# One sum of x1's blocks given to VectorE earlier in each turn: ahead of the tanh products instead of behind the gate's last sums

## The chip, the cores and the metric

The kernel runs on one core of a Trainium2 chip (trn2). The metric is the device time of one execution in microseconds (us), as the median over several runs. Engines are named as in the profile: PE is TensorE's matmul, PEld its weight load, DVE is VectorE, ACT is ScalarE, POOL is GpSimd, SP is SyncE, which issues the DMAs here. L240 is line 240 of the kernel.

## The reference, cut to what matters

Two layers of a graph network over 128 graphs of 64 nodes, with 768 features, all in float32:

```python
# layer 0: 12 heads of 64 features
h    = einsum('bnd,ade->bane', x, W)
th   = tanh(h)
attn = leaky(th @ w_src + transpose(th @ w_dst));  masked by adj;  softmax
out  = elu(einsum('banm,bame->bane', attn, h) + b)
gate = sigmoid(x @ H_w.T + H_b)
x1   = layernorm(x + gate * out + (1 - gate) * x)
# layer 1: 6 heads of 128 features
q, k, v = x1 @ Wq + bq, x1 @ Wk + bk, x1 @ Wv + bv
y    = softmax(q k^T / sqrt(128), masked by adj) v @ Wf + bf
x    = layernorm(x1 + y)
```

## The kernel before, in words

**Tiles and pairs.** A tile is 128 rows, that is two graphs. Layer 0 works on pairs of tiles, 32 pairs in all. A pair's two tiles are called t0 (first) and t1 (second) where the pair is the old one, n0 and n1 where it is the new one. Layer 1 begins when the last pairs are through.

**Products in seven parts.** Each product of a pair with a 768 x 768 weight (`h` for the features of layer 0, `g` for its gate, `v` for the values of layer 1) is done as a 2 x 2 block product with seven block products in place of eight. They are numbered 1 to 7, so `v6` is block product 6 of the values. Some of them take sums of the operand's blocks. For the values the operand is x1, transposed (tile `x1T`, 128 partitions x 6 chunks x 256 rows; the columns up to 128 are t0, those behind are t1). With a11 and a12 the two halves of t0's features and a21, a22 those of t1, `block_sums` makes four sums on DVE, each 128x384 float32:

```python
            lambda: e.tensor_tensor(s1, a21, a22, ALU.add),        # L240
            lambda: e.tensor_tensor(s2, s1, a11, ALU.subtract),    # L241
            lambda: e2.tensor_tensor(s3, a11, a21, ALU.subtract),  # L242
            lambda: e2.tensor_tensor(s4, a12, s2, ALU.subtract),   # L243
```

The first sum, s1, takes t1 alone. The second, s2, takes t0 too, and it is the stationary operand of `v6`. s1 itself is that of `v5`. In the profile the four are `sv_v`; the same lines run on POOL for the input x of layer 0, there they are `sx_x`.

**The order of the work is written out by hand.** The kernel runs under a manual schedule: each engine executes its instructions in the order in which they are emitted, and waits for the others where data demand it. A turn of the main loop takes a new pair through `h` and `g` and the old pair (one behind) through the rest of layer 0 and the values. `TURN` is the order of the block products on PE in one turn, 21 positions from 0 to 20:

```python
TURN = [
    "h1", "h2", "u4", "u3", "h6", "g1", "h5", "h7", "g2", "g6", "h4",
    "h3", "g5", "g7", "v1", "v2", "g4", "v6", "g3", "v5", "v7",
]
```

(`u4` and `u3` are the values' last two block products of the pair before the old one.) `step` emits a block product and behind it the way out of the one before, the DVE or ACT instructions that take it from PSUM. Other work is put on positions: `was(pos, ...)` for the old pair, `at(pos, ...)` for the new. What has the same position is emitted in the order of the calls. Turns 0, 1 and 2 and the tail have other tables of positions (`FIRST_AT`, `SECOND_OLD`, `THIRD_AT`, `LAST_AT`); turns 3 to 31, 29 in all, take the positions as written.

**The steps of a turn that matter here**, with their positions:

- 8: `by_features(t1)` transposes x1 of t1 on PE and copies it into `x1T` on ACT (L966, L967). 11: the same for t0.
- 11: `products(n1)`, 12: `products(n0)`: tanh of h on ACT (L888), then a product with w_dst on DVE (L889) and one with w_src on POOL (L890).
- 13, 14: `terms` sums these per head on DVE (`sd`, L897), writes the result to DRAM (`dstd`, L899) and reads it back spread over the rows (`dd`, two DMAs, L902); `with_bias` adds a bias to h on POOL (L913) and moves parts of it by DMA (L918, L919).
- 12: `v_begins` names the operands of the values and the four sum tiles; it issues no instruction.
- 15: s1, s2, and the DMA that writes `x1T` to DRAM (L1055). 16: s3, and `logits(n1)`, which adds `dd` and `sd` on DVE (L926, `att`). 18: `masked(n1)` (L942 to L949) and `logits(n0)`. 19: s4 and `exps(n1)`. 20: `masked(n0)`.
- Early in the next turn: `exps` on ACT (L955), transposes of the probabilities on PE (`pTp`), `attend` (L987), and `features` on DVE (L1003, L1004), which frees the PSUM banks for the transposes of the other tile.
- In between POOL makes the sums of the next x (`sx_x`) and sums of weights for layer 1 (`wacc`, L366), a few in each turn.

Of the kernel before, what the change touches and what calls it, by code (L numbers as in the profile page):

```python
# [134 lines left out]
def kernel(  # L135
# [620 lines left out]
    with ExitStack() as ph, ExitStack() as ph_r:  # L756
# [349 lines left out]
        v_sums, carried = {}, {}  # L1106
        summing = sum_weights(sb)
        for p in range(NP + 1):
            q = p - 1
# [9 lines left out]
            def at(pos, ok, *acts, places=of_new):  # L1119
                if ok:  # L1120
                    plan.setdefault(places.get(pos, int(pos)), []).extend(acts)

            def was(pos, *acts):
                at(pos, old, *acts, places=of_old)

            def do(f, *args):
                return lambda: f(*args)
# [15 lines left out]
            was(7.5, do(gated, t0))  # L1143
            was(8, do(by_features, t1), do(stats, t0))
            was(9, do(normed, t0))
            was(12, do(v_begins))
            was(15, lambda: v_sums[q][0](), lambda: v_sums[q][1](), do(spill_features, q))
            was(16, lambda: v_sums[q][2]())
            was(19, lambda: v_sums[q][3]())

# [210 lines left out]
```

## Time and profile before

| what | value |
|---|---|
| median of 3 runs | 2896.88 us (2893.63 to 2897.95) |
| the profiled execution | 2895.01 us |
| its span | 2893.2 us |
| mean granted TensorE clock | 0.998 |
| PE busy | 2842.0 us (98%) |
| DVE busy | 1939.4 us (67%) |
| POOL busy | 1292.9 us (45%) |
| ACT busy | 1059.4 us (37%) |
| share of PE in the chain that ended last | 78% |
| share of DVE in that chain | 11% |

The profile is of one execution, 1.8 us shorter in its span than that execution's own time. Layer 0 fills about the first 1535 us of the span. A view of waits says which instruction an idle engine waited for; a view of the timeline gives start, length, engine, line, output and inputs of each instruction, with the idle time before it in brackets.

### The profile page before, as it was taken

How to read it: one execution, taken by the hardware profiler on the slowest of the kernel's cores; microseconds unless marked ns; L12 is line 12 of the kernel's file. 1: busy time of each engine (PE TensorE's matmuls, PEld its weight loads, DVE VectorE, ACT ScalarE, POOL GpSimd, SP SyncE). 2: the span in 40 equal slices, each digit the busy share in tenths (PEclk: the TensorE clock that was granted, in tenths of full speed). 3: DMA queues.
4: the chain of work that ended last, by engine and by line, in shares of the span. 5: the costliest groups of instructions: out<-in, count | busy, mean ns of one | idle time of the engine just before them, and what ended most of it. 6: DMA issues, size and time to landing. Idle time of an engine off the chain costs nothing.

```text
span 2893.2 us, 47876 instructions
## 1 busy us (share of the span) xinstructions
PE 2842.0 (98%) x18252; PEld 2072.5 (72%) x18252; DVE 1939.4 (67%) x3203; ACT 1059.4 (37%) x1896; POOL 1292.9 (45%) x1253
## 2 busy tenths in 40 slices
PE   8899999999999999999999999999999999999998
PEld 4565556666566556666668888888888888888886
DVE  7878888888878888787863545555545555554556
ACT  2444444444344444444433223333213333322332
POOL 3445444444545444233343445434545443444534
PEclk9999999999999999999999999999999999999999
DMA  5444444444444444333353434332223433223432
GB/s 181 132 154 145 140 145 146 152 154 150 135 153 156 136 150 138 112 116 105 126 199 89 123 96 111 109 90 80 84 80 111 110 102 93 70 84 94 110 88 74
DMA packets 322068, 348.73 MB, mean 121 GB/s; under 512 B 147888, under 2 KB 247216, under 8 KB 321840
## 3 DMA queue, kind: packets, MB, share of 16 engines
q1 hardware_dynamic: 321840, 345.66, 39.2%
q8 instruction: 146, 2.39, 0.4%
q14 instruction: 82, 0.67, 0.1%
HBM read 198.48 MB, written 122.29 MB: 111 GB/s over the span
## 4 chain that ended last, share of the span: by engine, by line
PE 78%; DVE 11%; DMA 3%; issue 3%; ACT 3%; POOL 2%; SPq 0%; POOLq 0%; DVEq 0%; ACTq 0%
PE z_k L447 9%; PE z_o L494 9%; PE z_q L447 8%; PE y_h L270 6%; PE y_k L447 6%; PE y_q L447 6%; PE y_o L494 6%; PE y_g L270 5%; PE y_v L270 5%; PE z_h L270 3%; PE z_v L270 3%; PE z_g L270 2%; PE sp L550 2%; PE cp L634 2%; DVE sd L897 2%
## 5 line engine op out<-in xcount | busy, mean ns | idle before, releaser
L574 ACT ACTIVATE sc<-sc 128x512 f32<-128x512 f32 x48 | 30.6, 638 | 615.2 <-DVE sc L571 615.2
L695 POOL TENSOR_TENSOR y<-y,bf_bc 128x768 f32<-128x768 f32 x64 | 114.7, 1813 | 290.5 <-DMA y<-x1d 290.5
L507 DVE TENSOR_TENSOR y<-y,z_o 128x256 f32<-128x256 f32 x320 | 127.3, 417 | 140.4 <-PE z_o L494 140.2
L494 PE MATMUL z_o<-wf,so 128*128 128x256 f32 x896 | 215.8, 383 | 2.3 <-DVE y L507 1.2
L447 PE MATMUL z_q<-xs,w_wq 128*128 128x256 f32 x896 | 213.5, 381 | 0.3 <-POOL xs L411 0.3
L411 POOL TENSOR_TENSOR so<-ctxT 128x256 f32<-128x256 f32 x224 | 159.8, 731 | 90.8 <-PE y_o L494 45.9
L447 PE MATMUL z_k<-xs,hw_wk 128*128 128x256 f32 x840 | 198.5, 379 | 0.0
L1017 POOL TENSOR_TENSOR x<-gate,x 128x768 f32<-128x768 f32 x64 | 119.3, 1865 | 152.0 <-ACT gate L1068 137.0
L494 PEld LDWEIGHTS z_o<-wf,so 128*128 128x128 f32 x896 | 167.2, 190 | 26.9 <-issue 2.0
L447 PEld LDWEIGHTS z_q<-xs,w_wq 128*128 128x128 f32 x896 | 168.7, 190 | 24.3 <-POOL xs L411 0.7
L322 POOL TENSOR_TENSOR rs_b<-ve_b,minus_half 128x1 f32<-128x1 f32 x64 | 40.4, 631 | 313.0 <-DVE ve_b L320 312.2
L890 POOL TENSOR_TENSOR th<-th,wsd 128x768 f32<-128x768 f32 x64 | 117.9, 1843 | 134.6 <-DVE th L889 133.7
L447 PEld LDWEIGHTS z_k<-xs,hw_wk 128*128 128x128 f32 x840 | 159.5, 190 | 21.7
L322 POOL TENSOR_TENSOR rs_a<-ve_a,minus_half 128x1 f32<-128x1 f32 x64 | 35.8, 560 | 309.9 <-DVE ve_a L320 309.9
L411 POOL TENSOR_TENSOR xs<-r,r 128x512 f32<-128x512 f32 x112 | 147.4, 1333 | 40.3 <-DMA r<-x1Td 28.9
L462 DVE TENSOR_TENSOR qT<-qT,z_q 128x512 f32<-128x512 f32 x96 | 65.9, 687 | 141.5 <-PE z_q L447 141.5
L270 PE MATMUL y_v<-wv,sv_v 128*128 128x384 f32 x384 | 136.3, 491 | 10.3 <-DVE sv_v L241 8.3
L270 PE MATMUL y_h<-w_wq,xT 128*128 128x384 f32 x384 | 136.5, 492 | 8.5 <-DMA w_wq<-in_w_dram 7.9
L462 DVE TENSOR_TENSOR kT<-kT,z_k 128x512 f32<-128x512 f32 x96 | 66.0, 687 | 112.8 <-PE z_k L447 110.7
L270 PE MATMUL y_v<-wv,x1T 128*128 128x384 f32 x384 | 137.4, 495 | 1.8 <-ACT x1T L967 1.0
L270 PE MATMUL z_h<-w_wq,sx_x 128*128 128x384 f32 x384 | 137.6, 495 | 0.2 <-DVE w_wq L216 0.2
L270 PE MATMUL z_v<-wv,sv_v 128*128 128x384 f32 x384 | 137.6, 495 | 0.0
(165 smaller groups left out, 6909.0 us busy)
## 6 DMA issues: line engine op xcount, KB each, us to landing
x<-in_x_dram SPq DMA_DIRECT2D x64, 384.0 KB, 3.7
dd<-dstd SPq DMA_DIRECT2D x128, 192.0 KB, 3.4
x1d<-x SPq DMA_DIRECT2D x64, 384.0 KB, 2.6
x1Td<-x1T SPq DMA_DIRECT2D x32, 768.0 KB, 4.4
vd<-v SPq DMA_DIRECT2D x64, 384.0 KB, 3.0
r<-x1Td SPq DMA_DIRECT2D x96, 256.0 KB, 3.5
v<-vd SPq DMA_DIRECT2D x384, 64.0 KB, 2.3
y<-x1d SPq DMA_DIRECT2D x64, 384.0 KB, 5.4
```

The costliest lines, as they stand in the source:

```text
L270: T.matmul(to[:, : self.n], lhsT, rhs, start=kc == 0 and not more, stop=kc == HK - 1, skip_group_check=more,)
L322: G.tensor_tensor(rstd, ve, minus_half, ALU.pow)
L411: G.tensor_tensor(t, self.of(x[0]), self.of(x[2]), x[1])
L447: T.matmul(b[:, half * W2 : (half + 1) * W2], w[:, kc, half * P : (half + 1) * P], x[:, kc, :], start=half == kc == 0 and not more, stop=k ...
L462: V.tensor_tensor(at, at, b.rearrange("p (h t) -> p h t", h=2), ALU.add if sign > 0 else ALU.subtract,)
L494: T.matmul(b[:, :W2], x[:, kc, :], w[:, kc, :], start=kc == 0 and not more, stop=kc == 1, skip_group_check=more,)
L507: V.tensor_tensor(at, at, self.banks[path][:, :W2], ALU.add if sign > 0 else ALU.subtract)
L550: T.matmul(self.sp_[gr * N : (gr + 1) * N, (i * 2 + a) * N : (i * 2 + a + 1) * N], qT[:, 2 * self.f + a, at], kT[:, 2 * self.f + a, at], s ...
L634: T.matmul(self.cp_[a][e, at], self.v_[rows, i, gr, e], self.scT_[rows, at], start=True, stop=True,)
L695: G.tensor_tensor(y, y, pools["bf"], ALU.add)
L890: G.tensor_tensor(th[:, 1, :], th[:, 1, :], wsd[:, 1, :], ALU.mult)
L1017: G.tensor_tensor(xp, st[t]["gate"], xp, ALU.mult)
```

## The change

One line of the turn's plan is split. The naming of the operands and s1 go to position 11, and since the call stands ahead of the call that puts `products(n1)` there, s1 is emitted ahead of it. s2 and the write of `x1T` stay at position 15.

```diff
             was(9, do(normed, t0))
-            was(12, do(v_begins))
-            was(15, lambda: v_sums[q][0](), lambda: v_sums[q][1](), do(spill_features, q))
+
+            was(11, do(v_begins), lambda: v_sums[q][0]())
+            was(15, lambda: v_sums[q][1](), do(spill_features, q))
             was(16, lambda: v_sums[q][2]())
```

The calls behind it stay as they are: `at(11, new, do(products, n1))`, then `was(11, do(by_features, t0))`. In turn 1 `SECOND_OLD` sends position 11 to 15 and position 15 to 16, in turn 2 `THIRD_AT` takes 2 from each position, and in the tail `LAST_AT` sends 11 to 12 and 15 to 15.

## The prediction

> **What bounds the kernel now.** I read the page first. Its first part says that PE is the bound:
>
> ```profile
> PE 2842.0 (98%) x18252; PEld 2072.5 (72%) x18252; DVE 1939.4 (67%) x3203; ACT 1059.4 (37%) x1896; POOL 1292.9 (45%) x1253
> ```
>
> So an edit on DVE can only win what PE still waits for. The view of PE's waits in the first 1550 us (layer 0) has this at its top (total us, times, longest):
>
> ```profile
> PE y_v L270 <- DVE sv_v L241: 8.3, 11, 1.7
> ```
>
> That is v6 waiting for s2, the largest wait of PE there. For DVE the same view shows where DVE itself is idle:
>
> ```profile
> DVE th L889 <- ACT th L888: 98.0, 62, 2.8
> ...
> DVE att L926 <- DMA dd<-dstd: 10.0, 6, 5.0
> ```
>
> The first is the product that the change puts s1 in front of: DVE sits idle before it, 98 us in 62 cases. The second will come back as a limit. Next the view of the sums' tile (ns: shortest, median, longest):
>
> ```profile
> L240 DVE TENSOR_TENSOR sv_v<-x1T x32: 811/1309/2005, 89.1 to 1518.1; 128x384 f32<-128x384 f32 x32
> L241 DVE TENSOR_TENSOR sv_v<-sv_v,x1T x32: 557/965/1921, 90.5 to 1519.1; 128x384 f32<-128x384 f32 x32
> L242 DVE TENSOR_TENSOR sv_v<-x1T x32: 541/549/883, 91.0 to 1521.9; 128x384 f32<-128x384 f32 x32
> ```
>
> The three are the same operation on the same shape, yet s1 (L240) takes 1.31 us and s3 (L242) 0.55. The timeline of one turn, DVE and then POOL, tells why (start, length, idle before):
>
> ```profile
> 720.82 0.55 DVE L866 TENSOR_TENSOR gate<-y_g,hb_bc 128x384 f32<-128x384 f32 x1
> 723.43 0.96 DVE L889 TENSOR_TENSOR th<-th,wsd 128x768 f32<-128x768 f32 x1 [2.07 <-ACT th L888]
> ...
> 729.74 1.74 DVE L897 TENSOR_REDUCE sd<-th 128x24 f32<-128x1536 f32 x1
> 731.40 1.77 DVE L240 TENSOR_TENSOR sv_v<-x1T 128x384 f32<-128x384 f32 x1
> 733.20 0.56 DVE L241 TENSOR_TENSOR sv_v<-sv_v,x1T 128x384 f32<-128x384 f32 x1
> ...
> 734.62 1.52 DVE L926 TENSOR_TENSOR att<-dd,sd 128x768 f32<-128x768 f32 x1
> ```
> ```profile
> 720.62 0.73 POOL L366 TENSOR_TENSOR wacc_k<-wacc_k,wadd_k 128x256 f32<-128x256 f32 x1
> ...
> 729.43 3.32 POOL L913 TENSOR_TENSOR h<-h,b_bc 128x768 f32<-128x768 f32 x2
> ```
>
> POOL's two L913 end at 732.75, and s1, begun at 731.40, ends at 733.17, 0.42 us later. So s1 stood still until POOL was through. At 721.37, where the change puts it, DVE has 2.06 us of idle time and POOL has just finished.
>
> **Part 1: s1 at its new place.** 32 instructions move, none is added, and no DMA: the write of x1T stays on position 15, so SP's queue keeps its order, and so do POOL's, ACT's and PE's. On DVE s1 passes both L889, h's way out (L851), both L897 and the way outs L866 and L867. Its waits: x1T of t1, copied by ACT by 718.71 in this turn, and the old s1's last reader, v5 of the turn before; both are past. Queued behind it is L889 of n1, which needs ACT's tanh, ended at 723.40. I read this gap in every turn: from turn 2 to turn 31 it is 1.86 to 2.76 us, and POOL has at most one L366 of 0.73 us in it. So s1 costs 0.55 there, at worst 0.55 + 0.73 = 1.28, below the smallest gap: nothing. In turn 1 it falls into an idle 3.09 us ahead of L926 (waiting for `dd`). In the tail it falls among the way outs of layer 1's query (L462), where DVE waits for PE. If the cover were gone, it would cost 0.55 to 1.3 us a turn.
>
> **Part 2: s2 takes s1's place.** s2 starts when s1 did. Is it then done 1.3 us earlier? No: POOL's L913 still runs. Having s1's shape, s2 should end where s1 ended, so it comes earlier by its own length, 0.56 to 1.92 us. (In the Trainium skill, "SBUF — State Buffer", section "Who interferes with whom", a DVE instruction with two SBUF inputs and a GpSimd instruction that reads SBUF exclude each other for a whole instruction, and whoever comes second waits. By that rule the wait is inherited by s2, which the row of 733.17 bears out; were s1 simply a slow instruction, s2 would win s1's whole length, and the sum below would be about 1 us larger.)
>
> For v6 I took from PE's timeline the distance between starts of consecutive block products in the 29 full turns and subtracted the smallest of the 29. Ahead of v6 the excess is 0.49, 0.70, 0.71, 0.42, 0.13, 0.79, 1.87, 0.69, 0.10, 1.16, 0.54 and 0.19 us in twelve turns, 7.8 in all; turns 1 and 2 wait 1.13 and 1.38. With s2 ending where s1 ended and v6 starting 0.15 behind it (as the waiting ones do), all is gone but 0.88 of the 1.87, where s1 itself ended late, at 780.74:
>
> ```profile
> 781.88 2.17 PE L270 MATMUL y_v<-wv,sv_v 128*128 128x384 f32 x6 [1.71 <-DVE sv_v L241]
> ```
>
> and 0.47 and 0.11 of turns 1 and 2. That is 7.8 + 2.5 - 1.5 = **8.8 us**. In 23 turns v6 is also 0.08 longer than other products (1.9 in all), since its weights, which are s2, can't be loaded ahead; I count 1.4 of it. PE wins **10.2 us** at v6.
>
> **Part 3: what is late next.** The largest other excess in PE's table lies at the transposes of t0's probabilities in the next turn: 0.14 in nearly every turn, up to 1.55 in some, 8.8 in all. That chain runs L926 of n1, leaky, L942 to L949, L926 of n0, ..., L955 on ACT, L851, L1003, L1004, and DVE is nearly gapless in it. If PE comes earlier and the chain doesn't, the transposes wait longer. The chain comes earlier by s2's length at most, but L926 can't start before `dd` lands. From the issues of `dd` and their times to landing (3.0 to 3.8 us) I get a lead for each turn, the time from landing to L926: in this turn it landed at 734.51, L926 began at 734.62. 15 of 29 turns have 0.35 or less. With excess after = the larger of 0.14 and (excess + won at v6 - lead), and n0's `dd` as a second limit:
>
> - given back, named by v6's time: 0.32 (226), 0.78 (319), 0.51 (412), 0.37 (688), 0.99 (782), 0.54 (1012), 0.12 (1059), 0.26 (turn 1): 3.9 us;
> - kept: turn 2 and those at 366, 828, 1104, whose lead is 0.8 us or more, and the last full turns, which have 0.14 there;
> - won in turns without a wait at v6, by the lead alone: 0.9 us.
>
> **The sum.** 10.2 - 3.9 + 0.9 = **7.2 us**. The profiled execution took 2895.0 (span 2893.2 and 1.8 around it), so 2887.8 on its own scale. The median shown is 2896.88, 1.9 above it; the forecast against it is 2896.88 - 7.2 = **2889.7 us**. The unknown sizes: s2 at its new place 0.55 (POOL idle) to 2.0 (s1's longest), which moves the sum by about 1 up and 2 down; the lead used from nothing to all. I take s1's end, the nearest row. The sum can't exceed 10.2 plus what stands at the transposes above 0.14 (4.8): 15 us.
>
> **The rivals.**
>
> *Given back at the transposes.* If dependence on `dd` is tighter than my leads say, what v6 wins is lost 20 us later. For it: in six turns DVE already waits for `dd`. Against it: leads of 0.6 to 1.7 us in turns with waits of 0.7 us and more (v6 at 366, 688, 828, 1012). With no lead used only some 1 us stays; with a third to a half of the leads, 3. Time 2893.9 (2891 to 2896).
>
> *The move reaches nothing.* s2 needs t0's copies as well; if these, not s1, held it, nothing would change: 2896.9. Against it: they end at 725.17, six us ahead of s2.
>
> *Slower: L926 lands in POOL's sums.* L926 too reads two SBUF tiles and takes 1.52 us beside an idle POOL and 2.24 beside the `sx` sums. With s1 gone from POOL's way the `sx` sums start earlier. In 17 of the 29 turns L926 of n1 still takes 1.52. If an `sx` sum is under way whenever `dd` lands, each pays 0.72: 12.2 us, and these turns' gain goes too; 4.5 stay elsewhere. 2896.9 + 12.2 - 4.5 = 2904.6. It decides from the point at which `sx` starts ahead of the landing. Against it: in most of these turns POOL then waits for a DMA of weights and has no `sx` sum to run.
>
> **How the numbers follow.** Forecast 0.55, given back 0.26, nothing 0.07, slower 0.12. A measurement of this kernel can tell about 0.2% from no change, that is 5.8 us: faster is below 2891.1, slower above 2902.7. Nearly all of the forecast (0.50) and a little of the second case (0.04) make faster 0.54; most of the slower case makes slower 0.10; 0.36 is left for the same. The range reaches from 2885 (most of the leads kept, no wait inherited) to 2900, into the slower case; some 0.05 lie below it and 0.12 above.
>
> **What would show it.** Step 1: L240 at 0.55 us in the gap ahead of L889, and L889 no later behind the tanh; wrong if L240 takes over 1 us there. Step 2: L241's median near s1's old 1.3 us, and the wait y_v on L241 down from 8.3 to some 1.5. Step 3: PE's excess at the transposes up by about 3 us, and more waits of L926 for `dd`. The forecast is wrong if that excess grows by 8 or more, or if L926 has its 2.24 us in more turns than before.

## The result, and the profile after

The changed kernel takes 2885.29 us (median of 7 runs, 2883.43 to 2890.02) against 2894.46 for the kernel before in the same rounds (7 runs, 2892.59 to 2897.95): ratio 0.9967, 95% interval 0.9958 to 0.9976, that is 9.2 us less (6.9 to 12.2 by the interval). 7.2 were forecast. The forecast time, 2889.7, is 4.4 too high, and the measured one lies at the lower end of the range: 2.4 of the 4.4 come from the kernel before, whose median over all seven runs is 2894.46 and not the 2896.88 of the first three, and 2.0 from the change being worth more than forecast. The prediction put that lower end at most of the leads kept and no wait inherited by s2. s2 does inherit the wait (below), so the time came near this end for other reasons.

PE's waits in the first 1550 us of the changed kernel (total us, times, longest), those of interest:

```profile
PE pTp L966 <- DVE rden L1003: 3.5, 5, 1.1
...
PE pTp L966 <- DVE fo L1004: 1.7, 10, 0.2
...
PE y_v L270 <- DVE sv_v L241: 1.0, 2, 0.7
```

v6's wait for s2 went from 8.3 to 1.0 us. The wait of the transposes (pTp) for DVE's `rden` grew; in the kernel before the same view has

```profile
PE pTp L966 <- DVE rden L1003: 1.2, 2, 1.0
```

DVE's own waits in the same stretch, in the changed kernel:

```profile
DVE th L889 <- ACT th L888: 86.5, 62, 2.3
...
DVE att L926 <- DMA dd<-dstd: 24.1, 29, 4.1
```

The idle time ahead of L889 shrank by 11.5 us, s1 now stands in part of it, and L926 waits for `dd` 29 times instead of 6. The sums' tile, changed kernel (ns: shortest, median, longest):

```profile
L240 DVE TENSOR_TENSOR sv_v<-x1T x32: 546/548/1540, 83.8 to 1503.9; 128x384 f32<-128x384 f32 x32
L241 DVE TENSOR_TENSOR sv_v<-sv_v,x1T x32: 814/1314/1998, 88.5 to 1509.4; 128x384 f32<-128x384 f32 x32
```

s1 fell from 1.31 to 0.55, s2 rose from 0.97 to 1.31: the wait for POOL changed its owner. The same turn as in the prediction, DVE and then POOL:

```profile
717.62 0.55 DVE L240 TENSOR_TENSOR sv_v<-x1T 128x384 f32<-128x384 f32 x1
719.78 0.96 DVE L889 TENSOR_TENSOR th<-th,wsd 128x768 f32<-128x768 f32 x1 [1.62 <-ACT th L888]
...
727.75 1.77 DVE L241 TENSOR_TENSOR sv_v<-sv_v,x1T 128x384 f32<-128x384 f32 x1
...
731.10 1.52 DVE L926 TENSOR_TENSOR att<-dd,sd 128x768 f32<-128x768 f32 x1 [0.65 <-DMA dd<-dstd]
```
```profile
725.78 3.33 POOL L913 TENSOR_TENSOR h<-h,b_bc 128x768 f32<-128x768 f32 x2
```

L240 lies in the gap with 1.62 us of idle time to spare behind it, and L889 is still released by ACT. L241 has the 1.77 us that L240 had, and ends 0.41 after POOL's two L913 (729.11; DVE 729.52). L926, which began 0.11 after its landing before, now stands 0.65 us waiting for it.

Layer 0 got faster by the whole 9.3 us: the first product of layer 1's query starts at 1480.2 us instead of 1489.5. Of that 5.0 remain in the profiled execution at the start of the last such product (2806.2 instead of 2811.2). That execution took 2890.02, the longest of the seven; 1.8 of what it lost is PE waiting for ACT (`cp`, 3.1 us instead of 1.3), the rest was not followed up. In the profiles below, layer 1 takes 1322 to 1325 us between the starts of its first and last `y_q` product, here 1326.

### The profile page after: what moved, and what is told of

Read it like the earlier page. It is cut to its first block, busy times and chain, and to the rows that moved or that the text cites. A ratio compares the mean times of both kernels' runs of the same rounds, so it can differ in the third digit from the quotient of the medians.

```text
span 2888.2 us, 47874 instructions
## 1 busy us (share of the span) xinstructions
PE 2840.2 (98%) x18252; PEld 2075.9 (72%) x18252; DVE 1924.9 (67%) x3203; ACT 1061.2 (37%) x1896; POOL 1303.5 (45%) x1253
## 4 chain that ended last, share of the span: by engine, by line
PE 80%; DVE 9%; DMA 4%; ACT 3%; issue 2%; POOL 1%; SPq 1%; POOLq 0%; DVEq 0%; ACTq 0%
PE z_k L447 9%; PE z_o L494 9%; PE z_q L447 8%; PE y_h L270 6%; PE y_g L270 6%; PE y_k L447 6%; PE y_o L494 6%; PE y_q L447 5%; PE y_v L270 5%; PE z_h L270 4%; PE z_v L270 3%; PE z_g L270 2%; PE cp L634 2%; PE sp L550 2%; PE x_g L270 2%
## 5 line engine op out<-in xcount | busy, mean ns | idle before, releaser
L890 POOL TENSOR_TENSOR th<-th,wsd 128x768 f32<-128x768 f32 x64 | 118.0, 1844 | 137.7 <-DVE th L889 137.7
```

The lines of the kernel that those rows point to most:

```text
L890: G.tensor_tensor(th[:, 1, :], th[:, 1, :], wsd[:, 1, :], ALU.mult)
```

## The experiments

All ratios are to the kernel before, with 95% intervals. "Excess" is the measure of the prediction: the distance of block products on PE above the smallest of the 29 full turns. Before, it was 9.9 us at v6 (7.99 ahead of it and 1.89 within) and 8.8 at the transposes; in the changed kernel 2.1 and 10.0.

**Theory.** s1 costs nothing in the gap; s2 inherits the wait for POOL but ends earlier by its own length; what PE wins at v6 is in part given back at the transposes because L926 cannot start before `dd` has landed. **Rivals.** The early naming of the tiles is part of the gain; s1 does cost something where it stands; the place does not matter as long as s1 is gone from in front of s2; the landing of `dd` does not matter.

**The naming alone** (e1_names_only):

```diff
-            was(11, do(v_begins), lambda: v_sums[q][0]())
-            was(15, lambda: v_sums[q][1](), do(spill_features, q))
+            was(11, do(v_begins))
+            was(15, lambda: v_sums[q][0](), lambda: v_sums[q][1](), do(spill_features, q))
```

> Only the naming of the operands (with the four sum tiles) goes to position 11; s1 stays at position 15. My theory (the gain comes from s1's instruction alone, which now runs in an idle gap of VectorE): no instruction moves, so the time is that of the kernel before, ratio 1.000 within 0.001, and PE's wait of y_v on L241 stays near 8 us. Rival (taking the tiles earlier changes which waits are emitted, and that is part of the gain): ratio 0.998 or lower with L240 still at 1.3 us.

Ratio 1.0001 (0.9992 to 1.0010); v6 waits 8.7 us for s2, L240 has its 1.31. The gain is s1's instruction alone.

**s1 twice, at both places** (e3_s1_twice):

```diff
-            was(15, lambda: v_sums[q][1](), do(spill_features, q))
+            was(15, lambda: v_sums[q][0](), lambda: v_sums[q][1](), do(spill_features, q))
```

> s1 is computed twice, at position 11 as in the changed kernel and again at position 15 as before it (the same sum is written twice). My theory (s1 at the new place costs nothing, all of the change is that s1 is gone from position 15): ratio to the kernel before 1.000 within 0.001, the second L240 at 1.3 us as before, L889 of n1 still released by ACT. Rival (s1 at position 11 does delay the tanh products or POOL, and the gain at v6 is net of that): ratio 1.001 to 1.004, by the 0.55 us that it would cost in up to 29 turns.

Ratio 1.0000 (0.9992 to 1.0009). DVE executes 32 sums more than before, and the time does not move. The view of waits of this kernel, DVE and then PE:

```profile
DVE th L889 <- ACT th L888: 82.3, 62, 2.1
```
```profile
PE y_v L270 <- DVE sv_v L241: 7.2, 10, 1.4
```

The idle time ahead of L889 fell from 98.0 to 82.3 us, since the added sums of 0.55 us stand in its place, and v6 waits 7.2 us again. s1 in the gap is free.

**No s1 at all** (e4_no_s1; s2 is a21 - a11, and v5 multiplies a21, so the values are others):

```diff
+            B[q][5] = t[:, :HK, P:]
+            s2 = B[q][6]
+            v_sums[q][1] = lambda: V.tensor_tensor(s2, t[:, :HK, P:], t[:, :HK, :P], ALU.subtract)
```

> s1 is left out altogether: s2 is computed from a21 alone, and v5 takes a21 in its place, so the values are those of another product. My theory (the gap hides s1 fully): the same time as the changed kernel, ratio to the kernel before 0.996 to 0.998. Rival (s1 still costs something where it stands now): ratio 0.995 or lower, up to 0.55 us in each of 32 turns less than the changed kernel, that is 0.991 at the lowest.

Ratio 0.9971 (0.9960 to 0.9982), the changed kernel's within the intervals. Both sides agree within the intervals, which reach some 3 us to either side: adding s1 in the gap costs nothing, and taking it out of the gap wins nothing that they can tell. (In the one profiled execution layer 1 begins 1.7 us earlier than in the changed kernel's, at 1478.5 instead of 1480.2.)

**s1 behind the tanh products of n1 instead of ahead** (e2_s1_behind):

```diff
-            was(11, do(v_begins), lambda: v_sums[q][0]())
+            was(11, do(v_begins))
...
             at(11, new, do(products, n1))
+            was(11, lambda: v_sums[q][0]())
```

> s1 at position 11 as in the changed kernel, but emitted behind the tanh products of n1 instead of ahead of them. My theory (it is the idle gap ahead of L889 that makes s1 free, and POOL's L890, which starts when L889 ends, holds s1 up behind it): L240 has a median of 1.5 to 2 us instead of 0.55, L851 and the next L889 wait behind it, L897 of n1 begins 0.4 to 0.8 us later behind L889 of n1 than 3.6, dd lands that much later, and the ratio to the kernel before is 0.999 to 1.003: the gain is lost. Rival (any place ahead of L897 will do, VectorE has idle time ahead of the second L889 too): ratio 0.997 as for the changed kernel.

Ratio 0.9978 (0.9968 to 0.9987): some two thirds of the gain stay, so the expectation that it is lost was wrong. The interval alone would also allow the rival's 0.997; in the profiles layer 1 begins at 1483.6 us, 5.9 earlier than before the change, where the changed kernel's begins 9.3 earlier. DVE, then POOL, in this kernel:

```profile
723.56 0.96 DVE L889 TENSOR_TENSOR th<-th,wsd 128x768 f32<-128x768 f32 x1 [2.09 <-ACT th L888]
724.44 0.55 DVE L240 TENSOR_TENSOR sv_v<-x1T 128x384 f32<-128x384 f32 x1
...
727.41 1.74 DVE L897 TENSOR_REDUCE sd<-th 128x24 f32<-128x1536 f32 x1
```
```profile
724.60 2.07 POOL L890 TENSOR_TENSOR th<-th,wsd 128x768 f32<-128x768 f32 x1 [3.15 <-DVE th L889]
```

I had expected POOL's L890 to hold s1 up. It is the other way round: L240 stands directly behind L889 on DVE and is first, POOL comes 0.16 us later and takes 2.07 us instead of 1.82. L897 then starts 3.85 us behind L889 in most turns instead of 3.60, and `dd` lands 0.25 later behind L889 too, as the median of the 43 landings (of 58) that can be read; single ones move by up to 1.1 us either way. The place does matter, by a quarter of a microsecond a turn and not by 0.4 to 0.8.

**`dd` replaced by a tile that is always there** (e5a_before_dd on the kernel before, e5b_after_dd on the changed one; the DMAs still run, layer 0's attention is computed from other numbers):

```diff
-            sd, dd = st[t].pop("sd"), st[t].pop("dd")
+            sd, dd = st[t].pop("sd"), wsd[:, 0, :]
+            st[t].pop("dd")
```

> The kernel before, but L926 adds a constant tile (a row of w_dst, same size and strides) in place of dd; the DMAs that write dd run as before, nobody reads them, so L926 never waits for a landing and layer 0's attention is that of other numbers. My theory: before the change L926 seldom waits (10 us in all, 5 of them in one turn), so little is won: ratio to the kernel before 0.996 to 0.999. Rival (dd's landing holds the turn in both kernels alike): ratio 0.994 or lower.

> The changed kernel with the same constant tile in place of dd. My theory (behind v6 it is dd's landing that eats part of what s1's move wins: L926 waits 24 us in all and PE's excess at the transposes stays at 10 us): without that wait the lead reaches the transposes, their excess falls below 4 us, and the ratio to the kernel before is 0.991 to 0.994, so that the change is worth more here (0.004 to 0.006 against e5a) than with dd (0.0033). Rival (the landing does not matter to PE, the transposes are held by something else): the same ratio as the changed kernel, 0.9967, and the excess stays near 10 us.

Ratios 0.9994 (0.9985 to 1.0003) and 0.9943 (0.9931 to 0.9956). Without the wait for `dd` the change is worth 0.0051 instead of 0.0033, some 15 us instead of 9. Excess at v6 and at the transposes: 11.2 and 4.9 us without s1's move, 1.2 and 2.3 with it. So the move no longer pushes the transposes' excess up, it lets it fall; the landing is what takes a part of the gain back. Ahead of v7 the excess is 0.1 us in both of these kernels, against 2.3 before and 1.3 in the changed one. (Both ratios lie just above what I expected, 0.999 and 0.994. At the end of layer 0 PE waits 6.0 us in the first of the two kernels and 4.8 in the second for POOL's first sums of layer 1, 0.8 before the change; that these waits are the reason is not shown.)

**POOL's L913 left out** (e8_no_bias; layer 0's bias is missing):

```diff
-            G.tensor_tensor(
-                h[:, :, :E0], h[:, :, :E0], b01_bc.unsqueeze(1).to_broadcast([P, H0, E0]), ALU.add
-            )
```

> The changed kernel without L913, POOL's addition of the bias to h (layer 0's bias is left out; the DMAs that move parts of h stay). My theory (s2's 1.3 us are 0.55 of work and the rest a wait until POOL's L913 is through): L241 falls to a median near 0.56 us, and v6 has still more room; since v6 waits only 1.0 us in the changed kernel, the time falls by little through that, but L918 and L919 and with them dd of n0 come earlier too: ratio to the kernel before 0.993 to 0.997. Rival (s2 is slow where it stands for another reason, PSUM, the operand's layout or DMA traffic): L241 stays above 1 us.

Ratio 0.9951 (0.9937 to 0.9964). The sum s2 in this kernel:

```profile
L241 DVE TENSOR_TENSOR sv_v<-sv_v,x1T x32: 542/550/1284, 87.0 to 1505.3; 128x384 f32<-128x384 f32 x32
```

s2 is down to 0.55: its extra length was the wait for POOL's L913. PE's excess at v6 is 0.3 us, but at the transposes still 9.7: earlier sums only make DVE wait longer for `dd`, whose waits are now the third largest of DVE in layer 0:

```profile
DVE att L922 <- DMA dd<-dstd: 45.9, 37, 3.8
```

(L922 is L926 four lines up.)

**s2 moved up as well**, ahead of the tanh products of n0 (e7_s2_at_12):

```diff
-            was(15, lambda: v_sums[q][1](), do(spill_features, q))
+            was(15, do(spill_features, q))
...
             was(11, do(by_features, t0))
+            was(12, lambda: v_sums[q][1]())
```

> The changed kernel with s2 moved ahead too, to position 12 ahead of the tanh products of n0, behind t0's transposes. My theory: the second gap (0.9 to 1.1 us) is too short, since t0's copies end only some 0.8 us before the tanh and POOL's L890 of n1 runs there, so s2 delays the second L889 and L897 of n1, and with them dd: L897 begins 0.3 to 0.8 us later; v6 never waits, but the transposes' excess grows, ratio to the kernel before 0.997 to 1.000, worse than the changed kernel. Rival (only what stands ahead of s2 counts, and less work behind L897 of n0 is all gain): ratio 0.995 or lower.

Ratio 1.0001 (0.9992 to 1.0010): the whole gain is gone, though v6 never waits any more. DVE, then POOL:

```profile
586.93 1.93 DVE L241 TENSOR_TENSOR sv_v<-sv_v,x1T 128x384 f32<-128x384 f32 x1
588.78 0.94 DVE L889 TENSOR_TENSOR th<-th,wsd 128x768 f32<-128x768 f32 x1
589.65 1.74 DVE L897 TENSOR_REDUCE sd<-th 128x24 f32<-128x1536 f32 x1
```
```profile
586.62 1.82 POOL L890 TENSOR_TENSOR th<-th,wsd 128x768 f32<-128x768 f32 x1 [2.93 <-DVE th L889]
```

Here POOL's L890 is first, and s2 is held up until it ends (588.44) and delays the second L889, which has no wait for ACT left. In most turns L897 starts 4.06 us behind the first L889 instead of 3.60, `dd` lands 0.58 later in the median of the same 43 landings, and the transposes' excess is 20.1 us instead of 10.0. This is the price of a sum put where no gap covers it.

**s4 moved into the wait for `dd`** (e6_s4_early):

```diff
-            was(16, lambda: v_sums[q][2]())
-            was(19, lambda: v_sums[q][3]())
+            was(16, lambda: v_sums[q][2](), lambda: v_sums[q][3]())
```

> The changed kernel with s4 taken from position 19 to 16, between s3 and L926 of n1. My theory: VectorE now waits for dd there in most turns (24 us in all), so s4's 0.55 us is hidden in that wait, and it is gone from the chain between the two L926 and the transposes, whose excess of 10 us falls to 5 to 8: ratio to the kernel before 0.994 to 0.996, better than the changed kernel. Rival (s4 meets POOL's sums at the new place, or delays L926 where dd has landed already): ratio 0.997 to 0.998, no better or a little worse.

Ratio 0.9984 (0.9975 to 0.9992), worse than the changed kernel: the theory was wrong here. L926's waits for `dd` did halve (12.5 us), yet the excess at the transposes rose to 14.3. DVE and POOL in one of the last full turns:

```profile
1144.51 1.35 DVE L243 TENSOR_TENSOR sv_v<-x1T,sv_v 128x384 f32<-128x384 f32 x1
1145.78 2.23 DVE L926 TENSOR_TENSOR att<-dd,sd 128x768 f32<-128x768 f32 x1
```
```profile
1144.25 1.19 POOL L241 TENSOR_TENSOR sx_x<-sx_x,xT 128x384 f32<-128x384 f32 x1
1145.40 1.31 POOL L242 TENSOR_TENSOR sx_x<-xT 128x384 f32<-128x384 f32 x1
```

s4 takes 1.35 us and L926 2.23, since both run into POOL's sums of the next x. L926 of n1 is over 2 us long in 11 of 29 turns instead of 5 (in this turn the changed kernel has it too, 2.25; s4 it has later, and 0.55 us long as the median). That is the mechanism of the prediction's slower rival, seen here at work, where the change itself did not set it off.

**POOL's sums of x emitted later** (e10_sx_late), and the same **with s4 early** (e11_s4_early_sx_late):

```diff
-            at(17, p + 1 < NP, do(x_sums, p + 1), places={17: 12} if p == 0 else of_new)
+            at(19, p + 1 < NP, do(x_sums, p + 1), places={19: 12} if p == 0 else of_new)
```

> The changed kernel with POOL's four sums of the next x (sx) emitted at position 19 instead of 17. Each engine keeps its other work in place, but POOL's order changes: the sums come behind one or two more weight sums at most. My theory: POOL does not wait for positions, only for data, so the sums start about when they did and the two L926 and L949 meet them as before: ratio to the kernel before 0.996 to 0.998, like the changed kernel. Rival (the sums do come later, out of the way of L926 of n1): fewer L926 of 2.24 us than the 13 of the changed kernel and a ratio of 0.995 or lower.

> s4 at position 16 ahead of L926 of n1, as in an earlier run (ratio 0.9984, where L926 of n1 took 2.24 us in 11 turns instead of 5 and the transposes' excess was 14 us), together with the sx sums at position 19. My theory (s4 lost because s4 and L926 met POOL's sums, and position 19 does not move these in time): about the same loss, ratio 0.998 to 0.999. Rival (position 19 clears the way): 0.995 or lower.

Ratios 0.9962 (0.9949 to 0.9974) and 0.9970 (0.9958 to 0.9982). The first ratio lies in the range that I expected, but for another reason: position 19 does move the sums in some turns. One of them runs beside L926 of n1 in 9 turns instead of 13, L926 is over 2 us long 8 times instead of 13 (n1 and n0 together), and the transposes' excess is 7.5 us instead of 10.0. The median, 2884.79 us, is the lowest of the kernels that compute the reference, but its interval does not part it from the changed kernel's. With s4 early the ratio is 0.9970 instead of 0.9984, between theory and rival, and the intervals overlap; the excess fell from 14.3 to 10.5 us and L926 of n1 is over 2 us long in 8 turns instead of 11, which is the way that collisions would have it. s4 at position 16 still gains nothing over s4 at 19.

**The second read of `dd` on ACT's queue** (e9_dd_two_queues):

```diff
-                nc.sync.dma_start(
+                (nc.sync, nc.scalar)[g].dma_start(
                     out=dd[g * N : (g + 1) * N, :],
```

> The changed kernel with the second of the two DMAs that read dd back issued from ACT's queue instead of SP's, so that the two are issued together. My theory (the landing of dd sets L926 in most turns): it lands some 0.5 us earlier, L926's wait falls from 24 us to 10 or 15, the transposes' excess from 10 to 6 or 8 us, ratio to the kernel before 0.994 to 0.996. Rival (ACT, which then waits for the write of sd to land, holds up its own copies of v and the leaky step, or L926 begun earlier runs into POOL's sums): ratio 0.997 or higher.

Ratio 1.0361 (1.0346 to 1.0375), some 104 us slower. The theory was wrong, and what happened is the rival (ACT holds up its own copies of v), far larger than I had thought. ACT's and PE's largest waits in the first 1550 us:

```profile
ACT v L879 <- DMA dstd<-sd: 307.1, 29, 12.2
```
```profile
PE y_v L270 <- ACT v L879: 81.8, 29, 4.4
```

A DMA in ACT's order waits for the write of `sd` to land, and every copy behind it waits along, 10.6 us a turn on average; PE waits 81.8 us for such copies. The granted clock was lower too, 0.985 to 0.989 in the four runs against 0.997 to 0.998 in the kernel before beside them; how much of the 104 us that is was not followed up. This does not test the landing; the pair with `dd` replaced does.

## Why the prediction was right or wrong

**Which step failed.** The mechanism held; the sum did not. Two of its terms and its starting value were mis-sized: part 3 had PE lose 3.0 us at the transposes, and it lost 1.2; the end of layer 0 stood in the sum with nothing, though PE waited 2.0 us there, and 1.0 was won; and the kernel before was put at 2896.88, a median of three runs, where seven runs give 2894.46. In the profiles the terms come to 9.5 us instead of 7.2.

**What bounds the kernel, and part 1 (s1 is free in the gap): right.** L240 takes 0.55 us in 30 of its 32 places, L889 is released by ACT as before, and s1 added or removed at that place does not move the time.

**Part 2 (s2 ends where s1 ended, 10.2 us at v6): right in mechanism and size.** s2's median is 1.31, as s1's was. PE's excess at v6 fell by 7.8 us in the full turns, and those begin 1.9 us earlier through turns 1 and 2: 9.7. Leaving L913 out shows that s2's extra length is POOL's.

**Part 3 (3.9 us given back at the transposes, 0.9 won there): right in mechanism, mis-sized.** Net 3.0 us were to be lost there, 0.26 of them in turn 1; measured in the 29 full turns are 1.2 (8.8 to 10.0). By turns, named by v6's time: the seven that were to give back 3.6 gave back 2.65; the eleven others without a wait of over 0.13 at v6 won 0.1 together and not 0.9 (five won 1.2, four lost 1.1, which was not followed up); the last eight and those at 366 and 828, counted with nothing, won 1.4. Two things were missed. I took the 0.14 us that stand there in nearly every turn as a floor, "the larger of 0.14 and ...". It was none, and the kernel before shows it: four of its turns have 0.01 or less. In the last eight full turns, where L926 had 0.7 us or more of lead, it went to 0, 1.1 us in all. And I let the chain come earlier by the lead at L926 of n1 only. In the turn of 1012, which was to end with 1.3 us at the transposes and ended with 0.13, L926 of n1 came 1.05 us earlier behind L889 and was 0.2 shorter, L926 of n0 came 1.3 earlier, and L949 of n0 ended 1.9 earlier; it took 0.96 us instead of 1.26, since it no longer met one of POOL's weight sums. Collisions that shift are in no sum of leads. Turns that I took as held by `dd` (319 and 782, forecast 1.40 and 1.23) came out at 1.45 and 1.31.

**The end of layer 0: not in the sum.** In the last full turn PE's wait ahead of v7 (for ACT's L879) fell from 2.0 to 0.5 us, with L926's wait for `dd` (5.0 to 4.1); 0.5 came up ahead of v7 in the turn of 782. That `dd` holds it fits the kernels without the wait for `dd`, where it is gone. v7 of the last full turn, before and after:

```profile
1477.53 2.20 PE L270 MATMUL y_v<-wv,sv_v 128*128 128x384 f32 x6 [1.97 <-ACT v L879]
```
```profile
1468.02 2.20 PE L270 MATMUL y_v<-wv,sv_v 128*128 128x384 f32 x6 [0.48 <-ACT v L879]
```

With the net 1.0: 9.7 - 1.2 + 1.0 = 9.5, beside the 9.3 by which layer 1 begins earlier.

**The rivals.** The giving back is real but smaller than that case's share; replacing `dd` shows that it costs 5 to 6 us of what the change could bring. The slower case did not come: L926 is over 2 us long in 13 of 58 cases instead of 21, but its mechanism showed when s4 was moved. **The number** was also held against a median of three runs that lay 2.4 us above that of seven.

## What to carry to other kernels

A stalled instruction's length is not its price: look for what it waits on (here another engine's instruction on the same memory) and ask who inherits the wait when it is moved away. A small step was free here in a gap that is longer than the step and closed by another engine (s1, 0.55 us in at least 1.86). Another one a position further, where the next gap was too short and POOL was running (s2 at position 12), took the whole gain back. And after the first wait is removed, follow the chain to the next resource that it meets, and check a "floor" by asking what holds it.

## What the runs showed of the hardware

Of the 128 sums of `sv_v` in the kernel before, 75 began while an instruction of POOL was running; 74 of them ended 0.41 or 0.42 us behind it, whatever their start, and the 53 others took 0.54 to 0.56 us. (The one exception overlapped POOL's L372 for 0.28 us and took 0.55.) The one that starts first runs, the other stands. A lead of 0.16 us was enough: right behind the first L889 on DVE the sum goes first and POOL's L890 pays (2.07 us instead of 1.82), one instruction later the sum pays itself (1.93 us). The Trainium skill, "SBUF — State Buffer", section "Who interferes with whom", says that the order of issue decides who blocks; the two runs with s1 and s2 behind L889 show both orders. A DMA issue that waits in ACT's queue held that engine for 307 us in 29 turns.
